# Projecting a graph layer's queries and keys four row tiles at a time, with the weights loaded first and more walk work in the first slots

## The chip, the cores and the metric

The kernel runs on one core of one Trainium2 chip. The metric is the device time of one execution in microseconds. Before the change it is 1722.71 us, the median of three runs (1722.7 to 1722.73). The profiled execution's span is 1720.4 us, and the mean clock granted to TensorE in it is 0.983 of full speed.

## What is computed

Two graph layers over N = 2708 nodes with D = 256 features, all in float32. `S` is the dense 2708 x 2708 adjacency.

```python
# layer 0, steps n = 0, 1:
q = X @ W1.T @ W2.T ; k = X @ W3.T           # N x 64
probs = softmax(q @ k.T)                     # N x N
A = rows of probs cut to the top 90 % of their mass, renormalised
R = (S + I) / rowsum
Xf = R @ Xf ; Xa = A @ Xa                    # the "walk" and the attention
Z += Xf @ U1[n].T + Xa @ U2[n].T
h = layernorm(X + Z) * g + b ;  x = layernorm(x + h)
# layer 1: a four-headed graph attention with 64 features a head, masked by S != 0,
# then x = layernorm(x + heads)
```

The query projection is folded: `wq` = (W2 W1).T is formed once, so that each tile needs one product for q and one for k. Layer 1 needs `wx`, its W widened by eight columns that hold W times the attention vectors `a`.

## The kernel before

**Tiles.** The nodes form 22 row tiles, 16 of 128 rows and 6 of 110 (L71). Groups of up to four tiles of equal size (L75 to L80) are six: four of 4 x 128 rows, one of 4 x 110 and one of 2 x 110. `x` stays on the chip as `xe`, with a column of ones behind each row.

**Start (L466 to L550).** ScalarE's DMA queue issues, in this order: W3 twice (L476), four U matrices (L478), `g` (L479), `b` (L480), and later W1 (L537) and W2 twice (L539). SyncE's queue issues `x` (L93) and then the adjacency blocks of the walk. TensorE transposes W1 (L542), VectorE copies it (L543), and two products with W2 make `wq` (L546 to L550).

**Projections of step 0 (L989 to L993).** For each tile in turn, `turn` (L570) transposes its two halves into PSUM (L574) and copies them to SBUF as `xT` (L577, by VectorE on even and ScalarE on odd tiles). `project` (L552) multiplies `wq` and W3 with that `xT` (L559), 128 moving columns at a time; ScalarE copies q into `qT`, VectorE copies k into `kT`. `qT` has all nodes along its columns; in `kT` the first half of the nodes is on partitions 0 to 63 and the second on 64 to 127. All the projections have to be complete before the first row of scores, since each row needs all keys.

**Layer 1's weights (L965).** After the projections in program order, `layer1_weights` loads `gat_w` (L972) and `gat_a` (L975) by ScalarE's queue into a buffer of the three-deep pool of the big `e` rows, copies W to `wx` on POOL (L980), and forms the products with `a` on VectorE (L983, L984).

**The order written by hand (L995 on).** From here the engines' instruction order is the order in which Python emits it. `search` (L771) is a generator that carries one tile's attention row through scores (L580: matmul `lg` L591, exponential L595), search for the cut (MAX8 over pieces, L696; sorting rounds L714 and L716 in `settle`, L699), and weighting (`e`, L765). `walks` (L784) yields one walk matmul (L816) at a time, 22 for each of 22 tiles and each of two steps, out of adjacency blocks that are loaded a half tile ahead. At the end of a tile's 22, `after_walk0` (L825) adds the identity's row to the sum on VectorE (`xf`, L829), transposes it and multiplies it by U1 (`terms1`, L852); `after_attention0` (L838) does likewise for the attention, projects the keys and queries of step 1 and multiplies by U2 (`terms2`, L872). A `slot` (L931) moves every running search one piece on, may begin one, moves on the work in `doing`, and then spends walk matmuls:

```python
owed[0] += spend
while owed[0] > 0:
    owed[0] -= 1
    if next(stream, True):    # true at the end of a tile's walk
        break
```

What a break leaves owed is carried to the next slot. First come ten slots, the first without walk work and nine of `SPEND_FIRST` = 3, in which the searches of tiles 0, 1 and 2 begin (slots 0, 4 and 9). Then `step(0)` takes the 22 tiles' attention: `weigh` transposes each group of `e` (L172), ScalarE copies it (`eT`, L178), TensorE multiplies (L187), and a slot lies between groups: 11 walk matmuls a tile (`SPEND_0`), with tile t+3's search begun at the end of tile t. Slots of `SPEND_BETWEEN` = 6 then run for as long as `doing` holds anything; 13 more begin the searches of step 1; `step(1)` spends 28 a tile (`SPEND_1`). The end of a walk of step 1 leads to `finish` (L881), two layer norms and the sources of layer 1. A flag, which says whether all the searches held, is added up on VectorE (L1019 to L1053) and summed over partitions by one small matmul (L1057).

Of the kernel before, what the change touches and what calls it, by code (L numbers as in the profile page):

```python
# [8 lines left out]
F32 = mybir.dt.float32  # L9
# [7 lines left out]
P = 128  # L17
# [3 lines left out]
CHUNK = 512  # L21
# [12 lines left out]
NARROW = 26.0  # L34


SPEND_FIRST, SPEND_0 = 3, (2, 2, 2, 2, 2, 1)
SPEND_BETWEEN, SPEND_1 = 6, (5, 5, 4, 5, 5, 4)
HELD = 8
LN2 = 0.6931471805599453  # L40
# [5 lines left out]
def kernel(  # L46
# [16 lines left out]
    nc = tc.nc  # L63
    N, D = x.shape
    DA = w1T.shape[1]
    STEPS = u1T.shape[0]
    H, _, FO = gat_w.shape
    DC = D // P
    NT = (N + P - 1) // P

    rows = [P] * 16 + [110] * 6  # L71
    assert sum(rows) == N and len(rows) == NT
    off = [sum(rows[:t]) for t in range(NT + 1)]
    chunks = [(c, min(CHUNK, N - c)) for c in range(0, N, CHUNK)]
    groups = []  # L75
# [25 lines left out]
    xe = const.tile([P, NT, D + 1], F32, name="xe")  # L101
# [3 lines left out]
    ident = const.tile([P, P], F32, name="ident")  # L105
# [348 lines left out]
    def fast_layer0():  # L454

        l0 = ExitStack()
# [3 lines left out]
        HN = N // 2  # L460
# [8 lines left out]
        wq = w0.tile([P, DC, 2, DA], F32, name="wq")  # L469
        wk_sb = w0.tile([P, DC, 2, DA], F32, name="wk_sb")  # L470
        g_sb = w0.tile([P, D], F32, name="g_sb")
        b_sb = w0.tile([P, D], F32, name="b_sb")
        for h in range(2):
            nc.scalar.dma_start(wk_sb[:, :, h, :], w3T.rearrange("(c p) e -> p c e", p=P))
        load_x()
# [33 lines left out]
        qT = keep.tile([P, N], F32, name="qT")  # L509
# [6 lines left out]
        c2 = [dram.tile([P, D], F32, name=f"c2_{t}") for t in range(NT)]  # L516

        sortp = l0.enter_context(tc.tile_pool(name="sortp", bufs=1))
        heldp = l0.enter_context(tc.tile_pool(name="heldp", bufs=HELD))
        finp = l0.enter_context(tc.tile_pool(name="finp", bufs=2))  # L520
        ep = l0.enter_context(tc.tile_pool(name="ep", bufs=3))
        wk = l0.enter_context(tc.tile_pool(name="wk", bufs=1))
# [7 lines left out]
        ps_wk = l0.enter_context(tc.tile_pool(name="ps_wk", bufs=1, space=PSUM))  # L530


        tmp = ep.tile([P, N], F32, name="e")
        w1_raw = tmp[:, 0:P].rearrange("p (c e) -> p c e", c=DC)
        w2_sb = tmp[:DA, P : 2 * P].rearrange("p (h e) -> p h e", h=2)
        w1_sb = tmp[:DA, 2 * P : 4 * P].rearrange("p (c d) -> p c d", c=DC)
        nc.scalar.dma_start(w1_raw, w1T.rearrange("(c p) e -> p c e", p=P))  # L537
        for h in range(2):
            nc.scalar.dma_start(w2_sb[:, h, :], w2T)  # L539
        tr = ps_tr.tile([P, 4, P], F32, name="tr")  # L540
        for c in range(DC):
            nc.tensor.transpose(tr[:DA, c, :], w1_raw[:, c, :], ident)  # L542
# [1 line left out]
        for c in range(DC):  # L544
            tr = ps_tr.tile([P, 4, P], F32, name="tr")
            nc.tensor.matmul(  # L546
                tr[:, 0, :], w1_sb[:, c, :], w2_sb.rearrange("p h e -> p (h e)"),
                start=True, stop=True,
            )
            nc.vector.tensor_copy(wq[:, c].rearrange("p h e -> p (h e)"), tr[:, 0, :])  # L550

        def project(s, t, xT, copy_q, copy_k):  # L552

            m = rows[t]
            c0 = off[t]
            pj = ps_tr.tile([P, 4, P], F32, name="tr")
            for n, w in enumerate((wq, wk_sb)):
                for c in range(DC):
                    nc.tensor.matmul(  # L559
                        pj[:, n, :m], w[:, c].rearrange("p h e -> p (h e)"), xT[:, c, :m],  # L560
                        start=(c == 0), stop=(c == DC - 1),
                    )
            copy_q(qT[:, c0 : c0 + m], pj[:, 0, :m])
            low = max(0, min(HN - c0, m))
            if low:
                copy_k(kT[s][0:DA, c0 : c0 + low], pj[0:DA, 1, :low])
            if low < m:
                copy_k(kT[s][DA:P, c0 + low - HN : c0 + m - HN], pj[DA:P, 1, low:m])

        def turn(src, m, tp, copy):  # L570

            xT = rowp.tile([P, DC, P], F32, name="xT")
            for c in range(DC):
                nc.tensor.transpose(  # L574
                    tp[:, c, :m], src[:m, c * P : (c + 1) * P], ident[:m, :m]
                )
            copy(xT[:, :, :m], tp[:, 0:DC, :m])  # L577
            return xT
# [352 lines left out]
        def slot(spend, begin=None):  # L931

            advance(going)
            if begin and begin[1] < NT:
                going.append(search(*begin))
                next(going[-1])
            advance(doing)
# [3 lines that stand above are left out]
                if next(stream, True):  # L941
                    break
# [21 lines left out]

        def layer1_weights():  # L965

            tmp = ep.tile([P, N], F32, name="e")
            wg = tmp[:, 0 : DC * D].rearrange("p (c h o) -> p c h o", c=DC, h=H)
            ga = tmp[:, DC * D : DC * D + 2 * D].rearrange("p (h o) -> p h o", h=H)
            pr = tmp[:, DC * D + 2 * D : DC * D + 3 * D].rearrange("p (h o) -> p h o", h=H)  # L970
            for c in range(DC):
                nc.scalar.dma_start(  # L972
                    wg[:, c], gat_w[:, c * P : (c + 1) * P, :].rearrange("h p o -> p h o")
                )
            nc.scalar.dma_start(  # L975
                ga.rearrange("p h o -> p (h o)"),
                gat_a.rearrange("h o u -> (h o u)").partition_broadcast(P),
            )
            for c in range(DC):
                nc.gpsimd.tensor_copy(wx[:, c, 0:D], wg[:, c].rearrange("p h o -> p (h o)"))  # L980
                for k in range(2):
                    lo = FO * (1 - k)
                    nc.vector.tensor_mul(pr, wg[:, c], ga[:, :, lo : lo + FO])  # L983
                    nc.vector.tensor_reduce(  # L984
                        wx[:, c, D + k * H : D + (k + 1) * H], pr, axis=AX.X, op=ALU.add
                    )


        for t in range(NT):  # L989
            tp = ps_lg.tile([P, 2, CHUNK], F32, name="lg")  # L990
            xT = turn(xe[:, t, 0:D], rows[t], tp[:, 0, :].rearrange("p (c m) -> p c m", m=P),
                      nc.scalar.copy if t % 2 else nc.vector.tensor_copy)
            project(0, t, xT, nc.scalar.copy, nc.vector.tensor_copy)  # L993
        layer1_weights()
        with tc.manual_schedule(engines=engines):  # L995
            for n in range(10):
                slot(SPEND_FIRST if n else 0, (0, n // 4) if n in (0, 4, 9) else None)
            step(0, xe, SPEND_0)
            while doing:
                slot(SPEND_BETWEEN)  # L1000


            for t in range(3):
                for n in range(6):
                    slot(SPEND_BETWEEN, None if n else (1, t))
                    if t == 2:
                        break
            step(1, ba, SPEND_1)
            owed[0] = 0
            while doing:  # L1010
                slot(NT)
# [237 lines left out]
```

The softmax here doesn't subtract the row's maximum and nothing guards it: scores larger than these inputs give would overflow.

## Time and profile before

| what | where it is read | value |
|---|---|---|
| time, median of 3 | the runs | 1722.71 us |
| span of the profiled execution | top of the page | 1720.4 us |
| TensorE waits for W1, and then W2 | waits of TensorE | 13.9 and 3.9 us |
| first exponential of step 0 | timeline | 54.69 us |
| first attention transposes of step 0 | timeline | 83.85 us |
| first scores of step 1, first attention of step 1 | timeline | 622.8 and 674.6 us |
| last attention of step 1 ends | timeline | 1304.2 us |
| layer 1's first weights (`pt`, L1168) | timeline | 1334.8 us |

The page gives each engine's busy time, the span in 40 slices, the chain of work that ended last, and the costliest groups of instructions. In the groups' rows one matmul in float32 counts as two instructions; a transpose counts as one. A wait is given with the instruction that released it. In the timeline a line is a run of like instructions on one engine: start, duration, engine, line of the kernel, operation, destination and sources, shape, and in brackets the idle time before it with its releaser. "ACTq" and "SPq" are the DMA queues that ScalarE and SyncE issue into. These waits of other engines belong to the stages that the change touches:

- SyncE's fourth load of `x` is issued at 9.28, 7.0 us after the third.
- The first `gat_w` load is issued at 11.95, `gat_a`'s data are there at 23.19.
- The searches of step 0 start at 54.69 with tile 0; its weighted row `e` is done at 69.02, and tile 1's sorting follows on VectorE.

### The profile page before, as it was taken

How to read it: one execution, taken by the hardware profiler on the slowest of the kernel's cores; microseconds unless marked ns; L12 is line 12 of the kernel's file. 1: busy time of each engine (PE TensorE's matmuls, PEld its weight loads, DVE VectorE, ACT ScalarE, POOL GpSimd, SP SyncE). 2: the span in 40 equal slices, each digit the busy share in tenths (PEclk: the TensorE clock that was granted, in tenths of full speed). 3: DMA queues.
4: the chain of work that ended last, by engine and by line, in shares of the span. 5: the costliest groups of instructions: out<-in, count | busy, mean ns of one | idle time of the engine just before them, and what ended most of it. 6: DMA issues, size and time to landing. Idle time of an engine off the chain costs nothing.

```text
span 1720.4 us, 24503 instructions
## 1 busy us (share of the span) xinstructions
PE 1624.2 (94%) x8434; PEld 1080.7 (63%) x8434; DVE 1221.5 (71%) x3681; ACT 771.1 (45%) x1345; POOL 450.9 (26%) x915
## 2 busy tenths in 40 slices
PE   5799999999999998999999999999995999999895
PEld 4577777777777776777787878777774332322332
DVE  2754555554555108888989999999891979888896
ACT  1233333333333236656676666766632544243241
POOL 0011111111111133322344444345433300440313
PEclk9899999999999999999999999999997999999998
DMA  6111011101111132212222233322213323232231
GB/s 162 33 45 45 26 42 43 42 24 43 42 39 42 41 104 65 62 48 70 78 81 81 68 84 84 84 56 72 73 39 115 95 83 92 86 97 77 73 84 32
DMA packets 153875, 113.92 MB, mean 66 GB/s; under 512 B 39898, under 2 KB 144094, under 8 KB 153742
## 3 DMA queue, kind: packets, MB, share of 16 engines
q1 hardware_dynamic: 145048, 101.88, 21.8%
q10 hardware_dynamic: 6582, 4.84, 1.0%
q0 software_dynamic: 2112, 5.55, 0.9%
q8 instruction: 68, 1.11, 0.3%
q14 instruction: 65, 0.53, 0.1%
HBM read 101.16 MB, written 11.09 MB: 65 GB/s over the span
## 4 chain that ended last, share of the span: by engine, by line
PE 70%; DVE 15%; ACT 6%; POOL 4%; DMA 2%; issue 2%; ACTq 0%; SPq 0%; POOLq 0%; DVEq 0%
PE att L187 20%; PE walk L816 16%; PE acc L1176 11%; PE acc L1183 6%; PE lg L591 4%; PE tr L172 3%; ACT e L595 3%; PE tr L559 2%; DVE cand L696 2%; PE tr L872 2%; PE tr L852 2%; DVE scr L762 2%; DVE e L765 1%; DVE scr L681 1%; DVE work L716 1%
## 5 line engine op out<-in xcount | busy, mean ns | idle before, releaser
L1168 DVE SCALAR_TENSOR_TENSOR pt<-r,tj,bar 128x1024 f32<-128x1024 f32 (+3 forms) x264 | 296.6, 1185 | 49.2 <-DMA v<-v 20.0
L616 ACT ACTIVATE junk<-e,minus,rth 128x2708 bf16<-128x2708 f32 (+1 forms) x88 | 232.8, 2646 | 33.5 <-POOL rth L648 32.7
L816 PE MATMUL walk<-xe,blk 128*128 128x257 f32 (+3 forms) x968 | 243.8, 385 | 0.0
L187 PE MATMUL att<-xe,eT 128*128 128x256 f32 (+3 forms) x968 | 233.4, 381 | 7.6 <-ACT eT L178 7.6
L187 PE MATMUL att<-ba,eT 128*128 128x256 f32 (+3 forms) x968 | 235.2, 384 | 5.0 <-ACT eT L178 5.0
L1176 PE MATMUL acc<-pt,v 128*64 128x512 f32 (+3 forms) x1056 | 229.8, 553 | 4.6 <-DVE pt L1168 4.6
L816 PE MATMUL walk<-yw,blk 128*128 128x256 f32 (+3 forms) x968 | 228.2, 381 | 1.7 <-ACT xw L886 1.7
L178 ACT COPY eT<-tr 128x512 f32<-128x512 f32 (+5 forms) x264 | 136.9, 536 | 193.8 <-PE tr L172 193.4
L816 PEld LDWEIGHTS walk<-xe,blk 128*128 128x128 f32 (+3 forms) x968 | 173.7, 187 | 64.9 <-issue 41.8
L816 PEld LDWEIGHTS walk<-yw,blk 128*128 128x128 f32 (+3 forms) x968 | 176.9, 186 | 42.2 <-issue 12.3
L696 DVE MAX8 cand<-e 128x8 f32<-128x170 f32 (+1 forms) x352 | 89.4, 323 | 146.8 <-ACT e L595 146.8
L187 PEld LDWEIGHTS att<-ba,eT 128*128 128x128 f32 (+3 forms) x968 | 172.6, 188 | 33.4 <-ACT eT L178 10.2
L187 PEld LDWEIGHTS att<-xe,eT 128*128 128x128 f32 (+3 forms) x968 | 171.0, 186 | 35.7 <-ACT eT L178 12.6
L595 ACT ACTIVATE e<-lg 128x1024 f32<-128x1024 f32 (+1 forms) x132 | 121.0, 921 | 133.3 <-PE lg L591 128.4
L1176 PEld LDWEIGHTS acc<-pt,v 128*64 128x64 f32 (+1 forms) x1056 | 73.6, 137 | 153.9 <-issue 110.5
L172 PE MATMUL tr<-ident,e 128*128 128x128 f32 (+3 forms) x968 | 139.0, 270 | 6.1 <-DVE e L765 4.9
L172 PEld LDWEIGHTS tr<-ident,e 128*128 128x128 f32 (+3 forms) x968 | 116.4, 139 | 30.9 <-issue 5.7
L1116 ACT ACTIVATE bar<-bar 128x1024 f32<-128x1024 f32 (+3 forms) x66 | 62.9, 955 | 144.7 <-DMA bar<-in_adjT_dram 127.6
L1183 PE MATMUL acc<-pt,bj 128*32 128x512 f32 (+3 forms) x1056 | 124.6, 549 | 0.0
L829 DVE TENSOR_TENSOR xf<-walk,xe 128x257 f32<-128x257 f32 (+1 forms) x22 | 9.4, 426 | 156.9 <-PE walk L816 156.9
L696 DVE MAX8 cand<-scr 128x8 f32<-128x97 f32 (+1 forms) x616 | 101.7, 244 | 0.0
L714 DVE MAX8 top<-work 128x8 f32<-128x128 f32 (+3 forms) x242 | 82.4, 340 | 8.3
(194 smaller groups left out, 2009.6 us busy)
## 6 DMA issues: line engine op xcount, KB each, us to landing
blk<-in_adjT_dram SPq DMA_DIRECT2D x32, 704.0 KB
bar<-in_adjT_dram SPq DMA_DIRECT2D x32, 512.0 KB
blk<-in_adjT_dram SPq DMA_DIRECT2D x32, 330.0 KB
blk<-in_adjT_dram SPq DMA_DIRECT2D x32, 320.0 KB
blk<-in_adjT_dram SPq DMA_DIRECT2D x12, 605.0 KB
bar<-in_adjT_dram SPq DMA_DIRECT2D x12, 440.0 KB
bar<-in_adjT_dram SPq DMA_DIRECT2D x16, 330.0 KB
c<-cs POOLq DMA_DIRECT2D x32, 128.0 KB, 2.9
```

Source lines behind the costliest of these rows:

```text
L172: nc.tensor.transpose(tr[: rows[t], q, :m], e[:m, off[t] : off[t + 1]], ident[:m, :m])
L178: copy(eT[:k, : len(grp), :m], tr[:k, : len(grp), :m])
L187: nc.tensor.matmul(acc, eT[: rows[t], q, :m], value(t), start=(t == 0), stop=(t == NT - 1),)
L591: nc.tensor.matmul(lg[:m, h, :w], qT[part, cols], kT[s][part, c0 : c0 + w], start=True, stop=True,)
L595: nc.scalar.activation(halves[:m, :, c0 : c0 + w], lg[:m, :, :w], AF.Exp, accum_out=zp[:m, n : n + 1],)
L616: nc.scalar.activation(junk[:m], e[:m], func, scale=rth, bias=minus1[:m], accum_out=acc)
L696: nc.vector.max(cand[:, n, :], src[:m, n * size : min(N, (n + 1) * size)])
L714: nc.vector.max(top[:, k : k + 8], work if k else flat)
L816: nc.tensor.matmul(ac[:m, :w], blk[: rows[j], j - j0, :m], cur[: rows[j], j, 0:w], start=(j == 0), stop=(j == NT - 1),)
L1168: nc.vector.scalar_tensor_tensor(pt[:k, :gw], r[:k, h, :gw], tj[:k, j, h : h + 1], mask, op0=ALU.max, op1=ALU.mult,)
L1176: nc.tensor.matmul(acc[h // 2][c][q * FO : (q + 1) * FO, :w], v[j][:k, h - 1 + q, :], pts[h - 1 + q][:k, c0 : c0 + w], **at,)
L1183: nc.tensor.matmul(acc[2][c][h * 32 : (h + 1) * 32, :w], bj[j][:k, h, :], pts[h][:k, c0 : c0 + w], **at,)
```

## The change

W1 and W2 are loaded first, into two buffers of the pool `heldp` (which is opened earlier for that) instead of an `e` buffer. The projections of step 0 go by groups of up to four tiles: eight transposes into one pair of PSUM banks, two copies into an `e` buffer (ScalarE the first 128 features, VectorE the others), and four matmuls of up to 512 moving columns, with one copy of q and one of k per group. The k copy, with its split at half of the nodes, becomes a function `keep_k` that `project` uses too, as step 1 still goes tile by tile. `layer1_weights` moves from ahead of the ten first slots to behind them, loads by SyncE's queue behind the first adjacency blocks, and works in the buffer `scr`. `SPEND_FIRST` rises from 3 to 5. The change is for a shorter start and for use of TensorE while it waits for the first searches.

```diff
-SPEND_FIRST, SPEND_0 = 3, (2, 2, 2, 2, 2, 1)
+SPEND_FIRST, SPEND_0 = 5, (2, 2, 2, 2, 2, 1)
...
+        heldp = l0.enter_context(tc.tile_pool(name="heldp", bufs=HELD))
+        tmp = heldp.tile([P, D], F32, name="xa1")
+        w1_raw = tmp[:, 0:P].rearrange("p (c e) -> p c e", c=DC)
+        w2_sb = tmp[:DA, P : 2 * P].rearrange("p (h e) -> p h e", h=2)
+        w1_sb = heldp.tile([P, D], F32, name="xa1")[:DA].rearrange("p (c d) -> p c d", c=DC)
+        nc.scalar.dma_start(w1_raw, w1T.rearrange("(c p) e -> p c e", p=P))
+        for h in range(2):
+            nc.scalar.dma_start(w2_sb[:, h, :], w2T)
         for h in range(2):
             nc.scalar.dma_start(wk_sb[:, :, h, :], w3T.rearrange("(c p) e -> p c e", p=P))
         load_x()
...
-        tmp = ep.tile([P, N], F32, name="e")
...
-        nc.scalar.dma_start(w1_raw, w1T.rearrange("(c p) e -> p c e", p=P))
-        for h in range(2):
-            nc.scalar.dma_start(w2_sb[:, h, :], w2T)
...
         def layer1_weights():
-            tmp = ep.tile([P, N], F32, name="e")
+            tmp = wk.tile([P, N], F32, name="scr")
...
-                nc.scalar.dma_start(
+                nc.sync.dma_start(
                     wg[:, c], gat_w[:, c * P : (c + 1) * P, :].rearrange("h p o -> p h o")
                 )
-            nc.scalar.dma_start(
+            nc.sync.dma_start(
                 ga.rearrange("p h o -> p (h o)"),
                 gat_a.rearrange("h o u -> (h o u)").partition_broadcast(P),
             )
...
-        for t in range(NT):
-            tp = ps_lg.tile([P, 2, CHUNK], F32, name="lg")
-            xT = turn(xe[:, t, 0:D], rows[t], tp[:, 0, :].rearrange("p (c m) -> p c m", m=P),
-                      nc.scalar.copy if t % 2 else nc.vector.tensor_copy)
-            project(0, t, xT, nc.scalar.copy, nc.vector.tensor_copy)
-        layer1_weights()
+        for grp in groups:
+            k = rows[grp[0]]
+            w, c0 = k * len(grp), off[grp[0]]
+            tp = ps_lg.tile([P, 2, CHUNK], F32, name="lg")
+            for c in range(DC):
+                for q, t in enumerate(grp):
+                    nc.tensor.transpose(
+                        tp[:, c, q * k : (q + 1) * k], xe[:k, t, c * P : (c + 1) * P],
+                        ident[:k, :k],
+                    )
+            e = ep.tile([P, N], F32, name="e")
+            xT = e[:, 0 : DC * CHUNK].rearrange("p (c n) -> p c n", c=DC)
+            nc.scalar.copy(xT[:, 0, :w], tp[:, 0, :w])
+            nc.vector.tensor_copy(xT[:, 1, :w], tp[:, 1, :w])
+            pj = ps_lg.tile([P, 2, CHUNK], F32, name="lg")
+            for n, wm in enumerate((wq, wk_sb)):
+                for c in range(DC):
+                    nc.tensor.matmul(
+                        pj[:, n, :w], wm[:, c].rearrange("p h e -> p (h e)"), xT[:, c, :w],
+                        start=(c == 0), stop=(c == DC - 1),
+                    )
+            nc.scalar.copy(qT[:, c0 : c0 + w], pj[:, 0, :w])
+            keep_k(0, c0, w, pj[:, 1], nc.vector.tensor_copy)
         with tc.manual_schedule(engines=engines):
             for n in range(10):
                 slot(SPEND_FIRST if n else 0, (0, n // 4) if n in (0, 4, 9) else None)
+            layer1_weights()
             step(0, xe, SPEND_0)
```

More of the change, by code (lines that the diff above doesn't have):

```diff
@@ L518, in fast_layer0 @@
         sortp = l0.enter_context(tc.tile_pool(name="sortp", bufs=1))
-        heldp = l0.enter_context(tc.tile_pool(name="heldp", bufs=HELD))
         finp = l0.enter_context(tc.tile_pool(name="finp", bufs=2))
@@ L530, in fast_layer0 @@
         ps_wk = l0.enter_context(tc.tile_pool(name="ps_wk", bufs=1, space=PSUM))
-        tmp = ep.tile([P, N], F32, name="e")
[L534 to L537, printed above, removed]
-        for h in range(2):
-            nc.scalar.dma_start(w2_sb[:, h, :], w2T)
         tr = ps_tr.tile([P, 4, P], F32, name="tr")
@@ L550, in fast_layer0, with keep_k @@
             nc.vector.tensor_copy(wq[:, c].rearrange("p h e -> p (h e)"), tr[:, 0, :])
+        def keep_k(s, c0, m, src, copy):
+            low = max(0, min(HN - c0, m))
+            if low:
+                copy(kT[s][0:DA, c0 : c0 + low], src[0:DA, :low])
+            if low < m:
+                copy(kT[s][DA:P, c0 + low - HN : c0 + m - HN], src[DA:P, low:m])
         def project(s, t, xT, copy_q, copy_k):
@@ L563, in project @@
             copy_q(qT[:, c0 : c0 + m], pj[:, 0, :m])
[L564 to L568, printed above, removed]
+            keep_k(s, c0, m, pj[:, 1], copy_k)
         def turn(src, m, tp, copy):
```

## The prediction

> **What bounds the kernel now.** I began with the busy shares and the chain of waits that ended last.
>
> ```profile
> PE 1624.2 (94%) x8434; PEld 1080.7 (63%) x8434; DVE 1221.5 (71%) x3681; ACT 771.1 (45%) x1345; POOL 450.9 (26%) x915
> ...
> PE 70%; DVE 15%; ACT 6%; POOL 4%; DMA 2%; issue 2%; ACTq 0%; SPq 0%; POOLq 0%; DVEq 0%
> ```
>
> TensorE works 1624 of 1720 us and makes most of the chain. The change removes no matmul columns, so it can gain only TensorE's idle time (96 us) and time in which it runs slowly. Next, the list of what TensorE waited for:
>
> ```profile
> PE tr L542 <- DMA e<-in_w1T_dram: 13.9, 1, 13.9
> ...
> PE tr L574 <- DVE xf L829: 10.5, 5, 8.1
> ...
> PE tr L546 <- DMA e<-in_w2T_dram: 3.9, 1, 3.9
> ```
>
> Two early gaps stand out: 17.8 us on W1 and W2, and 8.1 us on one walk sum. The timeline of the start (start, duration, instruction, wait before it):
>
> ```profile
> 7.97 0.45 ACTq L537 DMA_DIRECT2D e<-in_w1T_dram  x1
> 16.64 1.28 ACT L577 ACT_TABLE_LOAD   x1 [16.64 <-DMA e<-in_gat_w_dram]
> 21.28 1.06 PE L559 MATMUL tr<-xT,wk_sb 128*128 128x128 f32 x4
> 23.19 0.42 DVE L983 TENSOR_TENSOR e<-e 128x256 f32<-128x256 f32 x1 [2.64 <-DMA e<-in_gat_a_dram]
> 29.88 0.71 PE L559 MATMUL tr<-xT,wq 128*128 128x128 f32 x4 [0.30 <-ACT xT L577]
> 30.43 0.61 PE L559 MATMUL tr<-xT,wk_sb 128*128 128x128 f32 x4
> 54.69 1.02 ACT L595 ACTIVATE e<-lg 128x1024 f32<-128x1024 f32 x1 [0.80 <-PE lg L591]
> ```
>
> W1 is issued at 7.97, behind everything else, and lands at 13.88; VectorE stops 2.64 us for layer 1's `gat_a`, with tile 0's k copy behind it. Four pieces take 1.06 us at 21.28, 0.61 at 30.43: half rate at first. The projections then settle at 2.79 us per two tiles until 53.5. The first exponential starts at 54.69.
>
> The first searches, in the same view:
>
> ```profile
> 79.51 0.69 PE L574 MATMUL tr<-ident,xf 128*128 128x128 f32 x2 [8.08 <-DVE xf L829]
> 79.99 4.24 PE L816 MATMUL walk<-xe,blk 128*128 128x257 f32 x10
> ```
>
> The transposes of the first walk sum wait for VectorE's `xf`, which stands behind tile 1's sorting (VectorE 9.28 of 70-80 us busy, TensorE 1.92). Walk work can be absorbed here. Step 0's remaining part keeps TensorE at 196.8 of 200 us. At the end of step 1 VectorE is never idle from 1211 until tile 21's weighting:
>
> ```profile
> 1287.61 0.94 PE L172 MATMUL tr<-ident,e 110*128 110x110 f32 x8 [2.73 <-DVE e L765]
> 1288.80 3.63 PE L187 MATMUL att<-ba,eT 128*110 128x256 f32 x8 [0.24 <-ACT eT L178]
> ```
>
> So there VectorE sets the end, and TensorE is cold after 2.7 us of idleness (eight such pieces take 1.89 us at 1273).
>
> **What the Trainium skill says.** "TensorE: Matmul & The Clock Gate", Back-to-back issue gap: matmul time goes by columns. The trace agrees (0.107 us per 128-column piece, 0.43 per 512), so 512 columns save waits and no array time. The same page, Part 1: The HAM clock gate, says that the array starts at half rate and doubles after a window of some 3.4 us of sustained activity. Here it is slow from 19.0 to about 25.3, and a 2.16 us wait at 672 sufficed to drop it, while 1.23 us at 1613 did not. "DMA: Bandwidth & Descriptors", Queues, rings and completion order: engines serve their queues round-robin, each in order; so W1 ahead of 1 MB of U arrives earlier. "ScalarE: Activation LUTs", What ACT_TABLE_LOAD costs: about 1.28 us; measured 1.28.
>
> **Front: -14.** TensorE's order becomes, per group, 4 to 8 transposes, two copies one after the other (ACT, then DVE), and 4 matmuls of 512 columns, without overlap between groups. In ScalarE's queue the table load and first copy now stand behind the issue of `b_sb`, which comes after the second W3 half lands; with three W issues more ahead of it that issue moves from 7.58 to about 9.5, the table load ends near 11, and the copy takes 0.588, so the first matmul is near 11.5 (10 to 14). A full group has 4 matmuls of 512 columns, each of two pieces in the trace: 8 x 0.43 = 3.44 us, the same columns as 32 pieces of 128 at 0.107. Group 0 would pay 6.9 at half rate throughout; it warms on the way, say 5.8: done at 17.3. Each later full group: 8 transposes x 0.107 = 0.86; the hole until the first copy has landed, 0.588 and a hand-over like the 0.30 wait on L577 less what the second half of the transposes covers, 0.75 (the second copy runs beside the first matmul); then 3.43: 5.04 together, against 5.58 before. Three give 15.1, the 440-column group 4.4 and the 220-column one 2.3 (scaled by columns, with the same hole): first `lg` at 39.1, first exponential 1.0 later as before, 40.1 against 54.69: -14.6. The hand-over may cost more, so -14. Bounds: copies serialised in full and table load late, -11; warm from the start, -17.
>
> **First searches: -0.7, with 18 more walk matmuls.** Nine slots of 5 in place of 3 add 18 x 0.434 = 7.8 us of TensorE work (27 to 45). From the first `lg` to the first attention transposes I add TensorE's queue: 2.9 (scores) + 6.5 (15 walks) + 1.9 + 2.2 + 0.8 + 0.9 = 15.2; `xf` comes at 16.0, wait 1; then 0.2 + 3.5 + 1.7 + 4.3 + 1.9 + 1.7 for transposes, walks, scores and terms: 29.5, that is 28.5 after the exponential, against 29.2 (83.85 - 54.69). The 8.1 us gap and the slow clock after it (ten pieces took 4.24 us at 79.99, 2.32 elsewhere) hide the walk work. Layer 1's weights (3.4 us DVE) now precede tile 2's candidates, which have slack; their copies run on a POOL 26% busy, their loads behind adjacency blocks that are due later: nothing.
>
> **Step 0: 0.** Same instructions per tile, TensorE-bound.
>
> **Drain before step 1: -5.2.** The loop runs while a tile's after-work is pending, 6 walks a slot. Before, it starts at walk 269 = 12x22 + 5, reaches a tile end at 286, which adds after-work: 31 walks. Now it starts at 287 and meets no end: 19. 12 x 0.434 = 5.2 us in a stretch bound by TensorE.
>
> **First search of step 1: +0.9.** From its `lg` to the attention are 51.8 us (622.8 to 674.6), with 75 walks; now 78 (+1.3). VectorE's chain ends it, and starts about 2 us sooner against TensorE, since `xf` stands ahead; but TensorE idles about 3 us on that `xf` and runs its next 2 to 3 us at half rate. Taken +0.9; bounds -1.5 and +3.
>
> **End of step 1: +0.7 and +1.1.** Walks left for tile 21 fall from 8 to 2; about four of them lie on the path: -1.7. The validity flag's matmul (L1057) is now placed ahead of tile 21's first attention matmul, so TensorE waits for `total`, ready 3.6 us after the last weighting (1291.1 against 1287.5), where before the transposes and four copies filled 1.2: +2.4. The longer wait leaves it cold for longer: +1.1. I take +1.8 (0 to +3). After that finish and layer 1 are unchanged.
>
> Sum: -14 - 0.7 - 5.2 + 0.9 + 1.8 = -17.2, so 1722.7 - 17.2 = 1705.5.
>
> **Rivals.** *A, the above: 1705.5, chance 0.55.* *B, no new waits:* the front warms early (-16), the drain as above, step 1's first search -1.5, tail -1.7, searches -0.7: -25, 1697.6. For it: walk matmuls around the gaps may keep the clock; against: TensorE has gaps between groups already, and every gap over 2 us measured dropped it. Chance 0.20. *C, half the front is lost:* a late table load or a clock that stays low through two groups makes the front -7: 1712.5. For it: the four-at-a-time order has 1.6 us of transposes and waiting in every 5; transposes may not count as activity (the skill's Part 4: PE-mode transpose). Chance 0.18. *D, slower:* TensorE stays at half rate through all projections, since each group begins with transposes and a hole: so a full group takes 1.72 + 0.75 + 6.88 = 9.35: 11.5 + 6.9 + 3 x 9.35 + 8.1 + 4.1 = 58.7 to the first `lg`, whose four slow pieces bring the first exponential to 60.2 (+5.5). With the drain and searches as above and the two new waits at their upper ends, 5.5 - 0.7 - 5.2 + 3 + 3 = +5.6: 1728 (1725 with the waits at A's values). Against it: the projections before had 0.64 us of waits in 2.79 (23%) and ran at full clock in the window of 30 to 40 us (granted 1.00). Chance 0.07.
>
> ```profile
> 30.00:40.00 10.00, 9.11 (x75) 8.39 (x76) 3.30 (x12) 2.97 (x10) 0.00 (x0) 1.00 0.01 2
> 70.00:80.00 10.00, 1.92 (x11) 0.85 (x8) 9.28 (x43) 2.12 (x4) 0.19 (x1) 0.68 0.28 72
> ```
>
> (Two stretches in us: length, busy time of PE, weight loads, DVE, ACT and POOL, then granted clock, DMA share and GB/s. The second is the first searches'.)
>
> **How the numbers follow.** A is likeliest: 1705.5. The range takes in A with its unknown terms (front 3 either way, tail 2, first search 2, which rarely add up), C up to 1716 and B's slower half: 1696 to 1716. Left out are about 0.08 of B, 0.04 of C and all of D, 0.19. Faster by over 0.2% (3.4 us) are A, B and nearly all of C: 0.92; within 0.2% are C's worst end and D's best, 0.03; the rest of D, 0.05, is slower.
>
> **What would show it.** Right: first exponential near 40 (36 to 43); the 512-column matmuls at 0.43 a piece in groups 1 to 4; the 8.1 us wait on `xf` cut to about 1 with 18 more walks before the first attention; 12 fewer walks in the drain; the flag's matmul (L1057 before) ahead of tile 21's first attention matmul, with a wait on `total`. Wrong: clock 0.5 beyond group 1, first exponential past 50, new waits in ScalarE's queue for the table load, or attention of step 0 starting more than 29 us after the first exponential.

## The result and the profile after

The changed kernel takes 1698.37 us (median of four runs, 1697.23 to 1699.64) against 1722.7 us: a ratio of 0.9862, with an interval of [0.9845, 0.9879]. The prediction was 1705.5 with a range of 1696 to 1716. The measured time lies inside, but 7 us below the number, at rival B's figure of 1697.6. What follows asks which of its steps were right, and where the 7 us are.

TensorE's busy time fell by 3.9 us (1624.2 before), its idle time, the span less that, by 19.2. Its busy line, and the list of its waits:

```profile
PE 1620.3 (95%) x8306; PEld 1064.8 (63%) x8306; DVE 1219.5 (72%) x3660; ACT 767.9 (45%) x1324; POOL 433.6 (26%) x915
```

```profile
PE tr L542 <- DMA xa<-in_w1T_dram: 5.1, 1, 5.1
...
PE tr L577 <- DVE xf L832: 3.4, 4, 1.8
PE walk L1078 <- DVE total L1074: 3.3, 1, 3.3
```

The wait for W1 is 5.1 us in place of 13.9, W2's 3.9 us is down to 1.1, the longest wait for a walk sum is 1.8 in place of 8.1, and a wait for the validity flag's `total` is new. The chain of waits of this run is no use: its record breaks off after the last few instructions. So the timeline is read stage by stage (start, duration, engine, line, operation, wait before it):

```profile
8.91 1.28 ACT L1004 ACT_TABLE_LOAD   x1 [8.91 <-issue]
10.85 3.78 PE L1009 MATMUL lg<-e,wq 128*128 128x512 f32 x4 [0.98 <-ACT e L1004]
...
20.76 1.88 PE L1009 MATMUL lg<-e,wk_sb 128*128 128x512 f32 x4
...
42.10 1.03 ACT L598 ACTIVATE e<-lg 128x1024 f32<-128x1024 f32 x1 [0.73 <-PE lg L594]
...
57.45 0.44 PE L577 MATMUL tr<-ident,xf 128*128 128x128 f32 x2 [0.52 <-DVE xf L832]
...
71.12 1.04 PE L172 MATMUL tr<-ident,e 128*128 128x128 f32 x8
```

The first exponential is at 42.1 (54.7 before). Four pieces of 512 columns take 3.78 us at the start of group 0, at half rate, and 1.88 in group 1. Nothing of note holds TensorE between 42 and 71, where it stood still for 8 us before. The end of step 1, in the same view:

```profile
1261.79 0.94 PE L172 MATMUL tr<-ident,e 110*128 110x110 f32 x8 [0.88 <-DVE e L768]
1266.01 0.19 PE L1078 MATMUL walk<-ones,total 128*1 128x1 f32 x2 [3.28 <-DVE total L1074]
1266.13 3.53 PE L187 MATMUL att<-ba,eT 128*110 128x256 f32 x8
```

The flag's matmul stands ahead of tile 21's attention and waits 3.28 us, and the eight pieces behind it run at half rate (3.53 in place of 1.89).

I cut both traces at the same events, and did the same for every experiment below. The stages are: up to the first exponential (A); from it to the first attention transposes (B; they start at 84.07 in the kernel before, and 83.85, given above, is the weight load in front of them); from the scaling of step 0's last attention row to the first scores of step 1 (D, the drain); from those to the scaling of step 1's first row (E); from there to that of tile 20 (F); tile 21 (G); the rest, finish and layer 1 (H). Step 0 between B and D takes 519.2 to 519.7 us in every kernel.

| kernel | A | B | D | E | F | G | H | span |
|---|---|---|---|---|---|---|---|---|
| before | 54.7 | 29.4 | 19.3 | 80.8 | 579.6 | 21.2 | 416.0 | 1720.4 |
| after | 42.1 | 29.0 | 13.3 | 79.5 | 576.6 | 19.8 | 417.4 | 1697.3 |
| SPEND_FIRST 3 in after | 40.7 | 28.7 | 19.3 | 80.8 | 579.7 | 20.3 | 415.8 | 1704.5 |
| SPEND_FIRST 5 in before | 53.3 | 29.0 | 13.3 | 79.5 | 576.5 | 19.9 | 416.0 | 1707.0 |
| W1, W2 first in before | 52.4 | 29.6 | 19.3 | 80.8 | 579.8 | 18.7 | 417.0 | 1717.1 |
| layer 1's weights late in before | 53.1 | 28.9 | 19.3 | 81.9 | 579.7 | 20.0 | 415.3 | 1717.4 |
| tile by tile in after | 41.7 | 29.0 | 13.4 | 79.5 | 576.5 | 21.2 | 416.5 | 1697.1 |
| layer 1's weights early in after | 50.5 | 29.0 | 13.3 | 79.5 | 576.5 | 20.8 | 415.6 | 1704.6 |
| flag late in after | 41.1 | 29.0 | 13.3 | 79.5 | 576.5 | 15.1 | 419.5 | 1693.4 |
| U behind x in after | 41.6 | 29.0 | 13.3 | 79.5 | 576.6 | 20.8 | 415.6 | 1696.2 |
| the same, W2 ahead of x | 41.5 | 29.0 | 13.3 | 79.5 | 576.6 | 21.2 | 415.4 | 1696.1 |
| the same, and flag late | 41.4 | 29.0 | 13.3 | 79.5 | 576.5 | 15.1 | 419.9 | 1694.4 |
| the same, with idle matmuls | 37.8 | 29.0 | 13.4 | 79.5 | 576.5 | 15.1 | 418.0 | 1688.9 |
| SPEND_FIRST 6 in after | 41.4 | 32.8 | 15.9 | 79.6 | 572.3 | 23.3 | 416.1 | 1700.6 |

From before to after: A -12.6, B -0.4, D -5.9, E -1.3, F -3.0, G -1.4, H +1.4, together -23.1, the difference of the two spans; the medians differ by 24.3. D, E and F repeat within 0.2 us from kernel to kernel wherever the walk work is the same (but for one E of 81.9). B scatters by up to 1 us, A, G and H by 1 to 2.5 us between kernels with equal code in that stage. The last section shows where most of the scatter in A comes from, and the E of 81.9: TensorE's half rate does not last equally long in equal code.

### The profile page after: what moved, and what is told of

Same layout as the page of the kernel before. It is cut to its first block, busy times and chain, and to the rows that moved or that the text cites. A ratio compares the mean times of both kernels' runs of the same rounds, so it can differ in the third digit from the quotient of the medians.

```text
span 1697.3 us, 24178 instructions
## 1 busy us (share of the span) xinstructions
PE 1620.3 (95%) x8306; PEld 1064.8 (63%) x8306; DVE 1219.5 (72%) x3660; ACT 767.9 (45%) x1324; POOL 433.6 (26%) x915
## 5 line engine op out<-in xcount | busy, mean ns | idle before, releaser
L819 PE MATMUL walk<-xe,blk 128*128 128x257 f32 (+3 forms) x968 | 240.6, 382 | 0.0
L819 PE MATMUL walk<-yw,blk 128*128 128x256 f32 (+3 forms) x968 | 228.0, 381 | 1.8 <-ACT xw L889 1.8
L819 PEld LDWEIGHTS walk<-xe,blk 128*128 128x128 f32 (+3 forms) x968 | 173.0, 186 | 53.1 <-issue 29.3
L819 PEld LDWEIGHTS walk<-yw,blk 128*128 128x128 f32 (+3 forms) x968 | 176.7, 186 | 41.6 <-issue 11.5
L605 POOL TENSOR_TENSOR fact<-zp 128x1 f32<-128x1 f32 (+1 forms) x44 | 24.9, 566 | 329.2 <-ACT e L598 319.4
```

Of the source, the lines that this page charges most:

```text
L605: nc.gpsimd.tensor_add(z, zp[:m, 0:1], zp[:m, 1:2])
L819: nc.tensor.matmul(ac[:m, :w], blk[: rows[j], j - j0, :m], cur[: rows[j], j, 0:w], start=(j == 0), stop=(j == NT - 1),)
```

## The experiments

### Where the walk work went: SPEND_FIRST alone, both ways

```diff
-SPEND_FIRST, SPEND_0 = 5, (2, 2, 2, 2, 2, 1)
+SPEND_FIRST, SPEND_0 = 3, (2, 2, 2, 2, 2, 1)
```

> The changed kernel with SPEND_FIRST back at 3, all else as changed. Theory 1 (the 18 walk matmuls of the first slots are absorbed in the waits and the slow clock of the first searches and save TensorE time later, in the drain, -5.9, and through step 1, -4.3): the front stays (first exponential at 42.1) and the time is 1698.4 + 10 = 1708.5 (1707 to 1710). Theory 2 (only the drain's 12 walks come from them; the gain in step 1 comes from an earlier start): 1698.4 + 5.5 = 1704 (1703 to 1705).

It took 1707.13 us (0.9924 of before, [0.991, 0.9938]). The wait on `xf` is back at its full length, with the front as in the changed kernel:

```profile
65.44 0.69 PE L577 MATMUL tr<-ident,xf 128*128 128x128 f32 x2 [8.05 <-DVE xf L832]
```

The other way, the kernel before with 5:

> The kernel before with SPEND_FIRST = 5 alone. Theory 1 (walks absorbed, saved in the drain and in step 1): 1722.7 - 10.2 = 1712.5, first attention still at 83.9, first scores of step 1 at 616.8, last attention's scaling at about 1294. Theory 2 (the drain alone): 1717. If the 18 walks were not absorbed but only moved, first attention would be at 91 and the time near 1722.

It took 1710.32 us (0.9944, [0.993, 0.9957]), 10.4 less than before in the same comparison. Both agree with theory 1, and the table shows where: with 5, whatever the front, B is no longer, D is 5.9 us, E 1.3 and F 3.1 us shorter. So the additional walk matmuls ran in time in which TensorE had stood still, and 10.3 us came back later. Stage F is the part that the prediction had not counted at all.

Not all of that is walk matmuls. Counted in the traces, B takes in 17 more of them, and also a product with U1 that came after it before, as the walk is further along; TensorE's idle time in B falls from 8.4 to 0.8 us. Of walk matmuls D then has 11.5 fewer and G 6 fewer. E and F have as many as before, and F is shorter all the same. The views of stretch F, before and after: all engines, of which the first is TensorE; then the walk matmuls alone (L816, L819); then the products with U1 alone (L852, L855):

```profile
703.63:1283.20 579.57, 571.82 (x2803) 448.40 (x2804) 532.09 (x1989) 371.70 (x605) 232.84 (x520) 1.00 0.27 70
683.45:1260.08 576.63, 569.85 (x2799) 447.42 (x2800) 529.59 (x1979) 370.76 (x602) 232.21 (x518) 1.00 0.27 71
...
703.63:1283.20 579.57, 264.03 (x1119) 202.64 (x1120) 1.00 0.27 70
683.45:1260.08 576.63, 263.81 (x1119) 202.67 (x1120) 1.00 0.27 71
...
703.63:1283.20 579.57, 9.58 (x20) 3.33 (x20) 1.00 0.27 70
683.45:1260.08 576.63, 7.70 (x16) 2.64 (x16) 1.00 0.27 71
```

TensorE is busy for all but 7.8 us of F before and 6.8 after. What left F is one product with U1 (four of the pieces, 1.9 us), since the walk is further along when F begins, and 1.0 us of idle time, about the 1.08 us for which TensorE waited for `xT` at 798 before. The same counts stand in the runs with SPEND_FIRST alone.

How far does that go? One more walk matmul a slot:

```diff
-SPEND_FIRST, SPEND_0 = 5, (2, 2, 2, 2, 2, 1)
+SPEND_FIRST, SPEND_0 = 6, (2, 2, 2, 2, 2, 1)
```

> The changed kernel with SPEND_FIRST = 6: 54 walk matmuls before the first attention instead of 44 or 45, 25 in the drain instead of 19, 572 in step 1 instead of 585. Theory 1 (at 5 the first searches have no more idle TensorE time, and the drain's length follows from where its start falls in a tile's walk): first attention 3 to 4 us later after the first exponential, drain 3 to 5 us longer, step 1 about 5 shorter: time 1699 to 1702. Rival (more walk work is still absorbed there): time 1695 to 1697.

It took 1702.84 us (0.9896, [0.9881, 0.9911]), 4.5 more than the changed kernel. B grows by 3.7 us: ten more walk matmuls at 0.43 are 4.3, so nearly nothing was left to absorb. In the changed kernel TensorE is busy for 29.29 of 30.10 us there; before it was 21.92 of 30.35 (the views of stretches):

```profile
41.00:71.10 30.10, 29.29 (x126) 19.84 (x127) 26.28 (x95) 9.46 (x20) 9.96 (x12) 1.00 0.29 73
```

```profile
53.50:83.85 30.35, 21.92 (x87) 14.25 (x87) 26.64 (x100) 8.55 (x18) 4.06 (x7) 0.83 0.17 46
```

D grows by 2.5 us, as its start falls elsewhere in a tile's walk and 25 matmuls run in it, not 19. F falls by another 4.3, here with 9.5 walk matmuls fewer in it, but G takes 3.5 more, since TensorE now arrives ahead of VectorE:

```profile
1268.51 1.70 PE L172 MATMUL tr<-ident,e 110*128 110x110 f32 x8 [7.24 <-DVE e L768]
```

That is the limit which the prediction had put at the changed kernel: there VectorE does set the end of step 1. In the changed kernel the same wait is 0.88 us.

### The start: two gates, one behind the other

W1 and W2 first, all else as before:

```diff
+        tmp = heldp.tile([P, D], F32, name="xa1")
...
+        nc.scalar.dma_start(w1_raw, w1T.rearrange("(c p) e -> p c e", p=P))
+        for h in range(2):
+            nc.scalar.dma_start(w2_sb[:, h, :], w2T)
         for h in range(2):
             nc.scalar.dma_start(wk_sb[:, :, h, :], w3T.rearrange("(c p) e -> p c e", p=P))
...
-        tmp = ep.tile([P, N], F32, name="e")
...
-        nc.scalar.dma_start(w1_raw, w1T.rearrange("(c p) e -> p c e", p=P))
-        for h in range(2):
-            nc.scalar.dma_start(w2_sb[:, h, :], w2T)
```

> The kernel before with W1 and W2 loaded first into the small buffers, projections tile by tile, layer 1's weights in the old place. Theory 1 (VectorE's wait for gat_a in front of tile 0's k copy is a second gate at the same place, which still opens at about 20 to 23): first exponential at 50 to 54, time 1718 to 1722. Rival (the arrival of W1 and W2 is the only gate): TensorE starts at 5, first exponential at about 46, time 1714.

It took 1719.49 us (0.9994, [0.9986, 1.0002]): no change that can be told. The first exponential came at 52.4. TensorE begins its projections at 8.5, 11.9 us sooner than it did, and is stopped twice:

```profile
8.51 1.06 PE L559 MATMUL tr<-xT,wq 128*128 128x128 f32 x4
...
13.12 0.35 ACTq L975 DMA_DIRECT2D e<-in_gat_a_dram  x1
...
15.22 1.22 PE L559 MATMUL tr<-xT,wq 128*128 128x128 f32 x4 [4.37 <-ACT xT L577]
...
19.88 0.43 DVE L983 TENSOR_TENSOR e<-e 128x256 f32<-128x256 f32 x1 [11.23 <-DMA e<-in_gat_a_dram]
...
21.33 1.22 PE L559 MATMUL tr<-xT,wq 128*128 128x128 f32 x4 [4.03 <-DVE junk L566]
```

First ScalarE is still issuing layer 1's loads (to 13.5, and the table load after them), then VectorE waits 11.2 us for `gat_a`, with the k copies (`junk` in the trace) behind it. The other gate alone:

```diff
-            tmp = ep.tile([P, N], F32, name="e")
+            tmp = wk.tile([P, N], F32, name="scr")
...
-                nc.scalar.dma_start(
+                nc.sync.dma_start(
                     wg[:, c], gat_w[:, c * P : (c + 1) * P, :].rearrange("h p o -> p h o")
                 )
-            nc.scalar.dma_start(
+            nc.sync.dma_start(
                 ga.rearrange("p h o -> p (h o)"),
...
-        layer1_weights()
         with tc.manual_schedule(engines=engines):
             for n in range(10):
                 slot(SPEND_FIRST if n else 0, (0, n // 4) if n in (0, 4, 9) else None)
+            layer1_weights()
```

> The kernel before with layer 1's weights formed late (SyncE's queue, buffer scr), W1 and W2 still loaded last, SPEND_FIRST 3. Theory 1 (two gates one behind the other: taking away one of them leaves the other): projections start once W2 is there, near 18; first exponential at 49 to 52, time 1717 to 1720. Rival (gat_a alone was the gate): first exponential near 43, time near 1710.

It took 1718.83 us (0.9984, [0.9978, 0.9991]), with the first exponential at 53.1: W2 still arrives at 18.8, and TensorE's products start at 20.2. So neither gate alone brings A down by more than A scatters: by 2.3 and 1.6 us against the kernel before, by 1.0 and 0.3 against the run with SPEND_FIRST 5, whose start is the same. In the whole time they bring 1.2 and 2.6 us. Both together bring A down by 12.6. The same from the other side, the changed kernel with `layer1_weights()` ahead of the slots:

```diff
+        layer1_weights()
         with tc.manual_schedule(engines=engines):
...
-            layer1_weights()
```

> The changed kernel with layer 1's weights formed where they were before (ahead of the ten first slots; loads still in SyncE's queue). Theory 1 (VectorE's products with gat_a are a gate of their own in front of the projections' k copies): VectorE waits until gat_a lands, at about 25, with group 0's k copy behind it; TensorE idles from about 18 to 25; first exponential at 49 to 53, time 1698.4 + 7 to 10 = 1705 to 1709. Rival (W1 and W2 were the only gate, and VectorE has slack): first exponential at 41 to 42, time 1698 to 1699.

It took 1707.31 us (0.9922, [0.9909, 0.9936]), 9 more than the changed kernel; A is 50.5, the other stages are the same but for scatter.

```profile
20.17 0.43 DVE L986 TENSOR_TENSOR scr<-scr 128x256 f32<-128x256 f32 x1 [8.75 <-DMA scr<-in_gat_a_dram]
...
24.53 3.75 PE L1009 MATMUL lg<-e,wq 128*128 128x512 f32 x4 [6.35 <-DVE junk L555]
```

VectorE waits for `gat_a` until 20.2, its products take until 23.7, and only then come group 0's k copy and group 1's x copy, for which TensorE waits 6.35 us; its matmuls are then at half rate again (3.75).

### The four-tile projections

The changed kernel with the loop of before:

```diff
-        for grp in groups:
-            k = rows[grp[0]]
...
-            keep_k(0, c0, w, pj[:, 1], nc.vector.tensor_copy)
+        for t in range(NT):
+            tp = ps_lg.tile([P, 2, CHUNK], F32, name="lg")
+            xT = turn(xe[:, t, 0:D], rows[t], tp[:, 0, :].rearrange("p (c m) -> p c m", m=P),
+                      nc.scalar.copy if t % 2 else nc.vector.tensor_copy)
+            project(0, t, xT, nc.scalar.copy, nc.vector.tensor_copy)
```

> The changed kernel with the projections of before (tile by tile, 128 moving columns), all other parts as changed. Theory 1 (512 columns save waits and no array time: 2.79 us per two tiles against 5.3 per four, plus a slow clock at first in both): first exponential at 43 to 46, time 1698.4 + 1 to 4. Rival A (the grouping is what starts TensorE early): first exponential past 49, time above 1705. Rival B (tile by tile starts sooner, since one tile's copy is enough): first exponential before 42, time below 1698.

It took 1699.05 us (0.9874, [0.9859, 0.9889]; the changed kernel's is 0.9862). The first exponential is at 41.7, against 42.1, and 40.7 to 42.1 in the four kernels with the changed start. Neither theory 1 nor rival A; rival B's direction, though by less than A scatters. The grouping as such brings nothing that can be told:

```profile
8.76 1.06 PE L566 MATMUL tr<-xT,wq 128*128 128x128 f32 x4
...
12.27 0.61 PE L566 MATMUL tr<-xT,wq 128*128 128x128 f32 x4
...
28.00 0.71 PE L566 MATMUL tr<-xT,wq 128*128 128x128 f32 x4 [0.30 <-ACT xT L580]
```

Tile by tile costs a little more in the steady state (2.79 us for two tiles, so 5.58 for four, against 5.25 from 20.76 to 26.01 in the changed kernel), some 1.8 us over 22 tiles. But its first product needs one tile's copy alone and starts at 8.76 in place of 10.85, and it is at full rate from about 11.9, where the grouped one gets there at about 16.5.

### What sets the first product

U, `g` and `b` to SyncE's queue, behind x:

```diff
-                nc.scalar.dma_start(u_sb[:, k, :, s], u[s].rearrange("(c p) e -> p c e", p=P))
-        nc.scalar.dma_start(g_sb, ln_g.partition_broadcast(P))
-        nc.scalar.dma_start(b_sb, ln_b.partition_broadcast(P))
+                nc.sync.dma_start(u_sb[:, k, :, s], u[s].rearrange("(c p) e -> p c e", p=P))
+        nc.sync.dma_start(g_sb, ln_g.partition_broadcast(P))
+        nc.sync.dma_start(b_sb, ln_b.partition_broadcast(P))
```

> The changed kernel with the loads of U, g and b moved from ScalarE's queue to SyncE's, behind x. Theory 1 (the first copy of the projections waits for ScalarE's queue: b's issue at 8.4 and the table load of 1.28 behind it): the table load starts at about 4, the first 512-column matmul at 8.5 to 9.5 instead of 10.85, first exponential 1.5 us earlier, time 1697. Rival (x or wq comes last anyway): first matmul within 0.4 us of 10.85, same time.

It took 1699.48 us (0.9875, [0.986, 0.989]), the same as the changed kernel; theory 1 does not hold. The table load moved from 8.91 to 3.64, and yet the first product started later, at 11.43: W2 came at 8.30, not 7.4. The loads of x were now all issued by 6.6, not 10.2, so they probably took more of the transfers at that time; that this delayed W2 was not tested by itself. The prediction's reason for its start near 11.5, the table load, was not the only one holding it. Then W2 ahead of x as well:

```diff
-            nc.scalar.dma_start(w2_sb[:, h, :], w2T)
+            nc.sync.dma_start(w2_sb[:, h, :], w2T)
```

> The changed kernel with U, g and b behind x in SyncE's queue, and W2's two loads at the head of that queue, ahead of x. Theory 1 (in the run with only U moved, TensorE waited for W2 until 8.30, later than in the changed kernel, 7.41, so W2's landing among x's packets is the gate): W2 is there by 5.5, the first 512-column matmul starts at 8.5 to 9.5 (10.85 in the changed kernel), first exponential near 40, time 1696.5 to 1697.5. Rival (the first x tiles, now behind W2, or the slow clock are the gate): first matmul at 10.5 to 11.5, time 1698 to 1700.

1697.88 us (0.9864, [0.9849, 0.9879]). The first product is where the rival had it, the time a little under its range: the first x tiles are then the last to come.

```profile
2.96 0.61 PE L542 MATMUL tr<-ident,xa 128*64 128x128 f32 x2 [2.96 <-DMA xa<-in_w1T_dram]
...
6.57 0.91 PE L998 MATMUL lg<-ident,xe 128*128 128x128 f32 x3 [3.00 <-DMA xe<-in_x_dram]
...
10.56 3.78 PE L1009 MATMUL lg<-e,wq 128*128 128x512 f32 x4 [0.68 <-ACT e L1004]
```

W1 is there at 2.96; the order of TensorE's instructions puts x's transposes ahead of `wq`'s products, and the first projection starts at 10.56, 0.3 earlier.

### The flag at the end of step 1

The sums of the flag are issued in order after step 1's last tile, and its matmul behind the last walk's work:

```diff
             step(1, ba, SPEND_1)
+            good = small.tile([P, 2, NT], F32, name="good")
...
             owed[0] = 0
             while doing:
                 slot(NT)
+            pt = ps_wk.tile([P, CHUNK], F32, name="walk")
+            nc.tensor.matmul(pt[0:1, 0:1], total, ones, start=True, stop=True)
```

> The changed kernel with the validity flag's sums and its small matmul moved behind the last walk's work. Theory 1 (TensorE's 3.3 us wait for the flag's total lies on the path that ends step 1): tile 21 of step 1 takes 2.5 to 4 us less between its weighting and its scaling, time 1698.4 - 3 = 1695.4. Rival (the end of step 1 is set elsewhere, by the layer norms and the loads of layer 1 that follow): time 1698 to 1699.

It took 1695.44 us (0.9852, [0.9837, 0.9867]). G falls from 19.8 to 15.1:

```profile
1260.50 0.95 PE L172 MATMUL tr<-ident,e 110*128 110x110 f32 x8 [0.85 <-DVE e L768]
1261.69 1.98 PE L187 MATMUL att<-ba,eT 128*110 128x256 f32 x8 [0.24 <-ACT eT L178]
```

TensorE goes straight on, and at full rate after a wait of 0.85 us. So theory 1 holds for tile 21, where the new wait and the half-rate matmuls cost 4.7 us. H is 2 us longer than in the changed kernel. That is about its scatter, but all three kernels with the late flag have a longer H (418.0 to 419.9) than any other (415.3 to 417.4); the order of layer 1's first matmuls differs somewhat there, and what of it costs time stays open. That the total came out at theory 1's 1695.4 is in part luck, as A happened to be 1.0 us shorter in the traced run.

### Two versions beyond both kernels

The late flag together with the loads of the run before it:

> The previous kernel (W2 ahead of x, U behind it) and the late validity flag together. If the two savings lie in different stretches they add: 1695.4 less what W2 first alone gives, about 1693.5 to 1694. If the end absorbs the start's gain: 1695.4.

1696.82 us (0.9858, [0.9843, 0.9873]): no better than the flag alone. To it, nine idle matmuls while TensorE waits for loads:

```diff
+        warm = ps_wk.tile([P, CHUNK], F32, name="walk")
+        for _ in range(6):
+            nc.tensor.matmul(warm[:, :P], ident, ident, start=True, stop=True)
...
+        for _ in range(3):
+            nc.tensor.matmul(warm[:, :P], ident, ident, start=True, stop=True)
```

> The previous kernel with nine idle matmuls of the identity with itself (results unused), six ahead of W1's transposes and three ahead of the first x transposes, while TensorE waits for loads. Theory 1 (group 0's first products run at half rate only because TensorE had too little activity before): they run at full rate, 0.43 a piece, group 0 takes 3.5 to 4.5 instead of 6 to 6.6 us, first exponential 1.5 to 2.5 earlier, time about 1692. Rival (the clock rises only some time after the products begin, or transposes and short matmuls don't count): first exponential within 0.7 us of the previous kernel's, same time.

It took 1691.3 us (0.9837, [0.9819, 0.9855]; five runs, 1689.82 to 1696.28). Two of the five came at about 1696, without the gain; only one of the others was traced, so whether the clock stayed low in those two isn't shown. In the traced one:

```profile
2.11 2.93 PE L542 MATMUL walk<-ident 128*128 128x128 f32 x12 [2.11 <-POOL ident masks.py:199]
...
6.36 0.71 PE L549 MATMUL tr<-xa,xa 64*128 64x128 f32 x4
...
9.37 1.98 PE L1015 MATMUL lg<-e,wq 128*128 128x512 f32 x4 [0.67 <-ACT e L1010]
```

The products of `wq` take 0.71 where they took 1.19, and group 0's first four pieces 1.98 where they took 3.78. The first exponential comes at 37.8, 3.6 us sooner than without. This is the fastest kernel of the study.

## Why the prediction was right, and where its sum was off

Its main terms were right in mechanism: the front, the absorbed walk work and the drain. Two terms failed, those of the first search and of the end of step 1, by 8.4 us together; the front gave back 1.4, and so did layer 1. That the time fell on rival B's figure is luck. B had the front at -16, no new waits and -1.7 for the end; the front was -12.6, the wait for `total` did come, and the gain that made up for both, in F, is in neither account. Of the first search it was nearer the mark (-1.5).

**Front, -14 predicted, -12.6 measured.** The mechanism was right: it named the loads of W1 and W2 and VectorE's wait for `gat_a`, and the runs show that both had to go. The first product came at 10.85 where 11.5 was put. Group 0 was put at 5.8 and took 6.4; the later groups were put at 5.04 and took 5.25 and 5.36 (groups 1 and 2, from first product to first product). The hole was put at 0.75 with one copy; in groups 3 to 5 it lasts until VectorE's k copy is done (waits of 0.74 to 0.98 on L557). What was wrong beside it is the account of the parts: "512 columns save waits and no array time" was given 0.54 us a group; the run tile by tile shows the saving used up by the later start.

**First searches, -0.7 predicted, -0.4 measured, with the additional walk work absorbed.** Right, and shown both ways by SPEND_FIRST alone.

**Drain, -5.2 predicted, -5.9 measured.** Right. Beside 11.5 walk matmuls, one walk tile's transposes and a wait of 0.6 us ahead of them left this stretch.

**First search of step 1, +0.9 predicted, -1.3 measured.** This step failed. Up to the first attention transposes the time is the same, 51.8 and 51.9 us, with 78 walk matmuls in place of 75 as put. The prediction had TensorE wait about 3 us on `xf` and run at half rate for 2 to 3 us behind it. The wait was 1.79 us, and the 18 walk pieces behind it ran at full rate (0.22 a piece):

```profile
651.66 0.41 PE L577 MATMUL tr<-ident,xf 110*128 110x110 f32 x2 [1.79 <-DVE xf L832]
651.91 4.08 PE L819 MATMUL walk<-xe,blk 128*110 128x257 f32 x18
```

What went is idle time. The kernel before waits for `e` at these transposes, and is at half rate behind it; the run with SPEND_FIRST 3 in the changed kernel has the same wait and full rate behind it:

```profile
674.63 1.94 PE L172 MATMUL tr<-ident,e 128*128 128x128 f32 x8 [2.16 <-DVE e L765]
676.40 2.65 PE L187 MATMUL att<-ba,eT 128*128 128x256 f32 x8
...
659.64 1.06 PE L172 MATMUL tr<-ident,e 128*128 128x128 f32 x8 [2.16 <-DVE e L768]
660.94 1.99 PE L187 MATMUL att<-ba,eT 128*128 128x256 f32 x8 [0.24 <-ACT eT L178]
```

Both have E = 80.8, so the half rate cost E nothing here: at full rate TensorE only waits longer for the next `xf` (1.55 us, 0.44 before). In the changed kernel `e` is ready at 654.7, TensorE comes to the transposes at 655.8, and neither wait occurs.

**End of step 1, +1.8 predicted, -4.4 measured (F -3.0, G -1.4).** This step failed too, and it is the larger part. The failing sentence is "So there VectorE sets the end". VectorE has no idle time for the last 75 us before tile 21's weighting, and the conclusion was drawn that TensorE work taken out ahead of it is worth nothing but for the four matmuls of the last tile; tiles 1 to 20 got no term. But over those tiles TensorE is the busier engine, 571.8 of 579.6 us against VectorE's 532.1, and F fell by the 3.0 us of TensorE's time counted above.

In G, in this pair, the parts are these. The six walk matmuls that are gone were 2.6 us of TensorE's time, not 1.7. The wait for `total` was foreseen and came (3.28 us), but the wait for `e` fell from 2.73 to 0.88, so that TensorE's idle time grew by 1.2 us, not 2.4; why `e` came earlier against TensorE's work is not shown. And nothing came of the 1.1 us for a colder TensorE: the eight pieces of attention took 3.63 us before and 3.53 after, half rate in both. The -1.4 is no gain that repeats, though. G is 18.7 to 21.2 us in the four kernels with the walk work of before, 20.1 in the mean, and 19.8 to 21.2 in the six with that of after and the early flag, 20.6 in the mean. Where VectorE does limit the end, the run with 6 shows.

**Layer 1, 0 predicted, +1.4 measured**, within the scatter of that stage.

## What to carry to other kernels

Before giving a wait a price, ask what the same instruction, and those in order behind it, would wait for next: here two gates in front of the same work were worth no more than 1 to 3 us singly and 12.6 together. A stall behind another engine takes in independent work at no cost until it is full, and not beyond; the work comes back as time wherever its own engine is the limit, and that has to be looked for in every later stage, also in one where another engine shows no idle time. A small matmul that only reports something should not stand in order ahead of work on the path.

## What the runs showed of the hardware

- **The start runs at half rate, and the granted clock does not show it.** From 10 to 18 us the changed kernel's column of the granted clock reads 1.00, while its pieces of 512 columns take 0.86 us each until about 16.5:

```profile
10.00:18.00 8.00, 7.15 (x16) 3.44 (x16) 0.69 (x1) 1.36 (x3) 0.00 (x0) 1.00 1.12 285
```

- **How soon the rate doubles varies in equal code.** Four of the kernels have the same start, and their first projection product begins at 10.73 to 10.85. The first piece that is wholly at full rate begins at 14.05 (SPEND_FIRST 3), 14.94 (late flag), 15.24 (SPEND_FIRST 6) and 16.80 (the changed kernel). The first and the last of them:

```profile
10.73 3.48 PE L1009 MATMUL lg<-e,wq 128*128 128x512 f32 x4 [1.15 <-ACT e L1004]
14.05 1.88 PE L1009 MATMUL lg<-e,wk_sb 128*128 128x512 f32 x4
...
10.85 3.78 PE L1009 MATMUL lg<-e,wq 128*128 128x512 f32 x4 [0.98 <-ACT e L1004]
14.42 2.97 PE L1009 MATMUL lg<-e,wk_sb 128*128 128x512 f32 x4
```

From the end of group 0 to the first exponential all four take 24.9 us, so that nearly all of A's spread of 1.4 us among them comes from this. It would fit what the Trainium skill says in "TensorE: Matmul & The Clock Gate", Part 1: The HAM clock gate, of a free-running window of about 3.4 us, in which it matters where the first matmul falls; no run here shows the window itself, and the times lie further apart than the 0.5 us either way that the page gives for sustained matmuls. The idle matmuls began at 2.11, and full rate was there by 6.4.
- **The same wait does not always cost the rate.** Behind the 2.16 us wait for `e` in step 1, with equal code, TensorE ran at half rate at once (the kernel before), at full rate throughout (SPEND_FIRST 3 in after), or at full rate in the transposes and at half in the products (W1 and W2 first):

```profile
672.71 1.06 PE L172 MATMUL tr<-ident,e 128*128 128x128 f32 x8 [2.16 <-DVE e L765]
674.02 3.56 PE L187 MATMUL att<-ba,eT 128*128 128x256 f32 x8 [0.24 <-ACT eT L178]
```

With layer 1's weights late the half rate there lasted longest (1.94 and 3.78 us, wait 2.22); that is the E of 81.9. So the prediction's "every gap over 2 us measured dropped it" holds in the trace that it read and not in all of these. No wait of 1.79 to 1.81 us on `xf` in step 1 cost the rate, in nine kernels. The drop can also come late: behind the wait of 2.73 us before tile 21's transposes, these still ran at full rate (0.94 for eight of 110 columns) and the products behind them at half (3.63).
